# Layer 2 of a four-layer graph kernel: both sums of a pair 64 features wide side by side, the 65th factor in a PSUM bank of its own, and no idle matmuls from layer 1 on

## The chip, the cores and the metric

The kernel runs on one core of a Trainium2 chip. Its engines are TensorE (PE, with its weight loads shown apart as PEld), VectorE (DVE), ScalarE (ACT), GpSimd (POOL) and SyncE (SP, which issues most DMAs). TensorE takes its operands from SBUF and writes to PSUM, which has banks of 512 fp32 columns on 128 partitions. The metric is the device time of one execution in microseconds; the kernel before has a median of 1097.2 us over 3 runs.

## What is computed

`x` is 4096 x 64, `adj` a sparse 4096 x 4096 matrix whose pattern is symmetric and whose values are not. Four layers follow one another, each `x = x + layer(relu(layernorm(x)), adj)`. The change concerns layer 2 alone, aggregation on the Poincare ball:

```python
deg = jnp.maximum(adj.sum(axis=1, keepdims=True), 1e-08)
w = adj / deg
log_ij = _logmap(x[:, None, :], x[None, :, :], c)
agg = jnp.einsum('ij,ijc->ic', w, log_ij)
transformed = agg @ weight + bias
```

`log_ij` is, for every pair (i, j), a vector made of x_i and x_j with factors that depend on the pair. The kernel doesn't form the vectors. It finds one number t_ij for each pair (from the distance of the two points, so that t_ij = t_ji), weighs it by the adjacency, and sums over j the 64 features h_j of the scaled point and one further number z_j. So the sum for a row i has 65 entries: 64 features and a 65th factor. A short chain for each block of 512 rows makes `agg` out of them.

Layer 0 is `relu((adj @ h) @ W0.T + b)`, layer 1 is attention with a sigmoid of products q k, layer 3 counts the non-zeros of each row and weighs by powers of two.

## The kernel before

**Tiles.** 4096 rows are 8 blocks of 512 (W, NB) or 32 chunks of 128 (P, NC). A tile of the adjacency is 2 chunks of j (a group, G = 2) by 512 columns of i, 512 KB. Layers 0, 1 and 3 walk over 8 x 16 such tiles. Layer 2 uses the symmetry of t: its list `work` (line 1058) holds the block pairs (ib, J) with J >= ib, two halves each, 72 entries in all. 16 of them are on the diagonal (ib = J); the 56 others (`two`, listed in `twos`) serve both ways: t itself for the rows of block ib, and t transposed for the rows of block J. In what follows an entry is a *step*, its *own sum* goes to block ib and its *mirrored sum* to block J.

**Engines in a step of layer 2.** In the order of the data:
- `l2_dists` (line 1101): TensorE, products `LT`, `RT` (64 rows) and `LB`, `RB` (32 rows) into one of two PSUM tiles `mm`
- `l2_squares` (1120): ScalarE, `v = mm^2`
- `l2_clamps`, `l2_clamps_v` (1130, 1137): GpSimd clamps `v`; in 30 steps ("shared") it does 768 of the 1024 columns and VectorE does 256
- `l2_signs` (1146): TensorE, a small product on 2 rows
- `l2_first_logs`, `l2_roots`, `l2_inverses` (1157 to 1180): ScalarE, a logarithm and two exponentials
- `l2_coshs` (1182): VectorE, `t = max(mm, ..) + t`, after which the `mm` tile is free; `l2_logs` (1189): ScalarE; `l2_pairs` (1195): VectorE, the finished t
- `l2_weights` (1202): VectorE, `w = t * adj`
- `l2_turns` (1213): TensorE, 8 transposes of t into the two spare banks `tr`; `l2_weights2` (1246): VectorE, `w2 = tr * adj2`
- `l2_sums` (1278): TensorE, own sum, two matmuls of 512 columns
- `l2_sums2` (1299): TensorE, mirrored sum, four matmuls of 256 columns for each half
- `l2_gathers` (1316): after both halves of a block J, the mirrored sum is added to the store `others` (ScalarE for ib = 0, else VectorE).

The stationary operand of both sums is `HA`, 65 columns wide (64 features and the factor), and the sums lie on 65 partitions: the own one in bank `acc0`, the mirrored one in bank `acc1`. All of it is fp32, and every fp32 matmul but a transpose stands as two records in the profile.

After the last step of a block ib, `after2` (line 658) adds the own sum and what was gathered for that block (VectorE), transposes the 65 x 512 result by row (`by_row`, line 384), and goes on with a chain of small operations on all engines; `before3` follows it.

**What sets the order.** The program is written out by a planner (`in_turn`, line 778): every stage is a thread that says on which engine its next piece goes and when its inputs will be there, by a cost model (`Pace`, line 67), and the piece that can start first is issued next. Within layer 2 `in_steps` (line 1329) fixes the order of the stages on each engine. On TensorE, step for step: distances of the next entry, signs, mirrored sum (two entries behind), transposes (one behind), own sum (one behind). Chains such as `after2` are in a queue `tail` and go in between. An engine executes its instructions in the order of issue.

**Idle matmuls.** Where the planner expects TensorE to wait for 0.6 us or longer, `keep_warm` (line 793) issues products of the identity into a spare bank. It does so in layer 0 until the first attention product of layer 1 has been issued, and again from the loading of layer 2's tables until `third_part` (line 1383) opens layer 3. `third_part` also frees layer 2's buffers, `others` among them.

**Side by side.** Layer 0 and the first part of layer 1 use `pair_sum` (line 913): its two matmuls are 64 wide and go to partitions 0 to 63 and 64 to 127 of one bank. The rest of layer 1 uses `quarter_sum` (line 1021) with four products of 64 rows by 64 columns. Layer 3's counts (line 1425) have products `pick` of 128 rows by 32 columns in bf16, four to a bank.

Of the kernel before, what the change touches and what calls it, by code (L numbers as in the profile page):

```python
# [9 lines left out]
F32 = mybir.dt.float32  # L10
# [4 lines left out]
ALU = mybir.AluOpType  # L15
# [131 lines left out]
def kernel(ctx: ExitStack, tc: tile.TileContext, a: dict, out: bass.AP):  # L147
# [79 lines left out]

    HA = keep.tile([P, NC, D + 1], F32, name="HA")  # L230
    RT = keep.tile([P, N], F32, name="RT")
    LT = keep.tile([P, NC // 2, P], F32, name="LT")
    RB = keep.tile([P, N], BF16, name="RB")
# [26 lines left out]
    def later_constants():  # L260


        def patterns():
            yield "POOL", lambda: 60.0
            for t, one in [(t, 1.0) for t in rbs] + [(t, 0.25) for t in lbs]:
                POOL.memset(t, 0.0)
                for k in (1, 3):
                    POOL.memset(t[:, :, k, 1:2], one)

        def weights_of_ranks():  # L270


            yield "DVE", lambda: 150.0
            near_f = st["rows"].tile([P, P], F32, name="near_f", bufs=1)
# [25 lines left out]

        return patterns(), weights_of_ranks()
# [189 lines left out]
    def before2(ib, st):  # L491
# [30 lines left out]
        ACT.copy(HA[:, cs(ib), 0:D], hh[:, :, 0, :])  # L522
# [8 lines left out]
        DVE.tensor_add(HA[:, cs(ib), D : D + 1], v[:, :, 0, :], v[:, :, 1, :])  # L531
        for k in range(3):
            t = rt("r_t", [P, CB, 2, 1], BF16)
            DVE.tensor_copy(t, v)
# [120 lines left out]
        DVE.tensor_add(x[:, cs(ib), :], x[:, cs(ib), :], s)  # L655
        yield ON_V

    def after2(ib, acc, others, st):

        e = rows.tile([P, W], F32, tag="e", name="e")[0 : D + 1, :]  # L660
        if others is None:
            ACT.copy(e, acc[0 : D + 1, :])
        else:
            DVE.tensor_add(e, acc[0 : D + 1, :], others)
        st["acc_free"][0] = pace.latest
        ps = yield from by_row(e, D + 1)

        t = rt("l2", [P, CB, D])  # L670
        z = rt("r_n", [P, CB, 1])
        DVE.tensor_copy(z, ps[:, :, D : D + 1])
        h = HA[:, cs(ib), 0:D]
        hz = rt("r_sq", [P, CB, D])
        DVE.tensor_mul(hz, h, ps[:, :, 0:D])
        DVE.tensor_mul(t, ps[:, :, 0:D], Qc[:, cs(ib), :].to_broadcast([P, CB, D]))
# [8 lines left out]
        DVE.tensor_sub(t, t, hz)  # L685
        vT = columns[slot["now"]]
        yield from transposed(t, D, vT[0:D, :])
# [105 lines left out]
    def keep_warm(wait):  # L793


        if wait < WAIT or not spare or l1[0].get("dist") and "tables" not in opened or "third" in opened:
            return
        t = bank()
        cold = not pace.shape
        for _ in range(min(int((wait - 0.2) / 0.28), 24)):  # L800
            PE.matmul(
                t[:, 0:P], ident, x[:, 0:2, :].rearrange("p c d -> p (c d)") if cold else ident,
                start=True, stop=True,
            )
        emptied(t)


    st = {
        "h0": HA[:, :, 0:D],
        "dg": {}, "dg_done": {}, "acc_free": [0.0, 0.0], "dg_free": [0.0, 0.0],  # L810
    }
    rows_at = {}
    opened = {}
# [269 lines left out]
    def second_part():  # L1083
# [9 lines left out]
        w2["others"] = w2["pool"].tile([D + 1, N], F32, name="others", bufs=1)  # L1093
        opened["second"] = l1[-1]["summed"]

    def second_tables():
# [179 lines left out]
            d["weighed2"] = pace.latest  # L1276

    def l2_sums():
        for d in work:
            yield "PE", lambda: latest(d.get("weighed"), take(0, d))  # L1280
            if d["first"]:
                accs["l2"] = acc_tile(0)
                st["acc_free"][0] = None
            acc = accs["l2"]
            for c in range(G):
                PE.matmul(
                    acc[0 : D + 1, :], HA[:, d["g"] * G + c, :], d["w"][:, c, :],
                    start=(d["first"] and c == 0), stop=(d["last"] and c == G - 1),
                )
            d["summed"] = pace.latest  # L1290
            if d["last"]:
                ib = d["ib"]
                others = w2["others"][:, ws(ib)] if ib else None
                follow(
                    with_mark(3, ib, after2(ib, acc, others, st), before3(ib, None)),
                    ON_V if ib else ON_S, evicts=True,
                )

    def l2_sums2():
        for d in twos:  # L1300
            yield "PE", lambda: latest(
                d.get("weighed2"), 0.0 if d["half"] else st["acc_free"][1]
            )
            if d["half"] == 0:
                accs["turned"] = acc_tile(1)
                st["acc_free"][1] = None
            acc = accs["turned"][0 : D + 1, :]
            part = slice(d["half"] * G * P, (d["half"] + 1) * G * P)
            for k in range(CB):
                PE.matmul(  # L1310
                    acc[:, part], HA[:, d["ib"] * CB + k, :], d["w2"][:, k, :],
                    start=(k == 0), stop=(k == CB - 1),
                )
            d["summed2"] = pace.latest

    def l2_gathers():
        for d in twos:
            if d["half"] == 0:
                continue
            yield "DVE" if d["ib"] else "ACT", lambda: d.get("summed2")  # L1320
            o, acc = w2["others"][:, ws(d["J"])], accs["turned"][0 : D + 1, :]
            if d["ib"] == 0:
                ACT.copy(o, acc)
            else:
                DVE.tensor_add(o, acc, o)
            st["acc_free"][1] = pace.latest
            d["gathered"] = pace.latest

    def in_steps(*stages):
# [197 lines left out]
    def l3_sum():  # L1527
# [15 lines left out]
        if d["last"]:  # L1543
# [67 lines left out]
```

## Time and profile before

| what | value |
|---|---|
| median of 3 runs | 1097.2 us (1095.84 to 1097.63) |
| the profiled execution | 1093.92 us, span 1092.2 us, mean granted TensorE clock 0.988 |
| TensorE busy | 1038.4 us, 95% |
| VectorE busy | 929.7 us, 85% |
| ScalarE busy | 790.0 us, 72% |
| GpSimd busy | 260.2 us, 24% |
| layer 2's stretch, 459 to 905 us | TensorE 428.75, VectorE 410.93, ScalarE 382.56, GpSimd 179.62 of 446 us |
| layer 3's stretch, 905 to 1092 us | TensorE 178.02, VectorE 109.46, ScalarE 138.66, GpSimd 3.38 of 187 us |

How to read the lines below. A line of a timeline has the start in us from the span's start, the length in us, engine, source line, operation, written tile <- read tiles, shape and number of records merged into it; in brackets the idle time of that engine before it and what ended it. All operations go through one helper, so they all show line 139 and are told apart by their tiles. In a shape, `128*65` before a TensorE record is rows by columns of the stationary operand. A line of a stretch has start:end and its length, then busy time and number of instructions of PE, PEld, DVE, ACT and POOL, the granted TensorE clock (1.00 is full), the busy share of the DMA engines and their GB/s. A line of groups ends in busy time (union), mean ns of one, and the idle time ahead of it. TensorE's records overlap, and their ends are modelled, so distances between starts say more than lengths.

### The profile page before, as it was taken

The numbers are of one execution on the slowest core, as the hardware profiler recorded it, in microseconds if no ns is written. First come the engines' busy times: TensorE is split into PE (matmuls) and PEld (weight loads), VectorE is DVE, ScalarE is ACT, GpSimd is POOL, SyncE is SP. The second block draws the span as 40 slices with busy tenths as digits, with TensorE's granted clock in tenths as the row PEclk, the third lists the DMA queues.
The fourth block names the chain that finished last, engine by engine and source line by source line (L and its number), as shares of the span: only waits on it lengthen the run. The fifth ranks groups of instructions, "written<-read, shape, count | busy, mean of one in ns | idle before, by whom it ended". The sixth has DMA issues, their size and how long they took to land.

```text
span 1092.2 us, 16919 instructions
## 1 busy us (share of the span) xinstructions
PE 1038.4 (95%) x6032; PEld 464.3 (43%) x6032; DVE 929.7 (85%) x1522; ACT 790.0 (72%) x1228; POOL 260.2 (24%) x151
## 2 busy tenths in 40 slices
PE   7989999999999999999999999999999988999998
PEld 3334444333233333354454454444444444454444
DVE  7778999988999999888998999989899999665650
ACT  1144545466777777799989879888798777677776
POOL 3021312110110011243344344334343431000000
PEclk9899999999999999999999999999999999999999
DMA  8999999976687778544553553445536549999950
GB/s 288 405 360 408 398 380 379 310 238 218 208 281 265 240 263 274 171 143 173 181 184 118 179 206 116 174 154 174 174 122 209 191 154 380 376 409 409 410 221 10
DMA packets 76202, 271.77 MB, mean 249 GB/s; under 512 B 9046, under 2 KB 10070, under 8 KB 76118
## 3 DMA queue, kind: packets, MB, share of 16 engines
q1 hardware_dynamic: 75456, 270.57, 68.3%
q8 instruction: 47, 0.77, 0.3%
q14 instruction: 37, 0.30, 0.1%
q10 hardware_dynamic: 662, 0.13, 0.1%
HBM read 269.62 MB, written 1.05 MB: 248 GB/s over the span
## 4 chain that ended last, share of the span: by engine, by line
PE 54%; DVE 21%; issue 8%; ACT 6%; POOL 5%; DMA 4%; SPq 1%; ACTq 0%; DVEq 0%; POOLq 0%
PE acc L139 27%; PE mm L139 17%; PE tr L139 10%; DVE dg L139 5%; POOL v L139 4%; DMA adj<-in_adjT_dram 4%; DVE t L139 4%; DVE w L139 3%; DVE sig L139 3%; ACT sig L139 2%; ACT t L139 1%; ACT lo_sq L139 1%; ACT v L139 1%; DVE h L139 1%; DVE ln_v L139 1%
## 5 line engine op out<-in xcount | busy, mean ns | idle before, releaser
L139 PE MATMUL acc<-w,HA 128*65 128x256 f32 (+1 forms) x736 | 246.2, 470 | 8.6 <-DVE w L139 8.4
L139 POOL TENSOR_SCALAR v<-v 128x1024 f32<-128x1024 f32 (+1 forms) x72 | 171.1, 2376 | 253.3 <-ACT v L139 253.3
L139 ACT ACTIVATE sig<-mm,att_b,att_a 128x1024 f32<-128x1024 f32 x128 | 150.7, 1203 | 57.4 <-PE mm L139 53.5
L139 ACT ACTIVATE wt<-mm,down 128x1024 fp32r<-128x1024 f32 x128 | 136.0, 1110 | 40.0 <-PE mm L139 39.2
L139 DVE TENSOR_TENSOR sig<-sig,adj 128x1024 f32<-128x1024 f32 x128 | 152.7, 1220 | 10.6 <-ACT sig L139 10.4
L139 DVE TENSOR_TENSOR dg<-dg,adj 128x1024 f32<-128x1024 f32 x113 | 137.9, 1221 | 1.6
L139 PE MATMUL mm<-qT,kT 64*64 64x512 f32 (+1 forms) x896 | 130.2, 599 | 6.6 <-ACT sig L139 6.1
L139 PEld LDWEIGHTS acc<-w,HA 128*65 128x65 f32 x736 | 94.2, 138 | 92.0 <-issue 50.1
L139 PE MATMUL acc<-sig,HL 64*64 64x512 f32 (+1 forms) x896 | 130.0, 599 | 1.4 <-DVE sig L139 1.4
L139 PE MATMUL acc<-adj,HA 128*64 128x512 f32 x512 | 125.2, 623 | 5.7 <-DMA adj<-in_adjT_dram 5.4
L139 ACT ACTIVATE v<-v,minus 128x1024 f32<-128x1024 f32 x72 | 79.1, 1098 | 27.4 <-POOL v L139 26.3
L139 DVE SCALAR_TENSOR_TENSOR t<-mm,t 128x1024 f32<-128x1024 f32 x72 | 83.6, 1161 | 14.8 <-PE mm L139 11.0
L139 DVE SCALAR_TENSOR_TENSOR t<-t,v 128x1024 f32<-128x1024 f32 x72 | 83.3, 1157 | 3.4 <-ACT t L139 3.4
L139 DVE TENSOR_TENSOR w<-t,adj 128x1024 f32<-128x1024 f32 x72 | 84.4, 1173 | 1.4
L139 DVE TENSOR_TENSOR w<-tr,adj 128x512 f32<-128x512 f32 x120 | 77.5, 683 | 7.5 <-PE tr L139 7.2
L139 ACT ACTIVATE t<-t 128x1024 f32<-128x1024 f32 x72 | 72.2, 1003 | 12.0 <-DVE t L139 11.9
L139 ACT ACTIVATE v<-mm 128x1024 f32<-128x1024 f32 x72 | 69.6, 967 | 14.0 <-PE mm L139 14.0
L139 PE MATMUL mm<-RT,LT 64*128 64x512 f32 (+1 forms) x288 | 77.9, 618 | 0.0
L139 PE MATMUL acc<-wt,S 128*128 128x512 f32 x256 | 77.1, 426 | 0.6 <-ACT wt L139 0.5
L139 ACT ACTIVATE t<-v 128x1024 f32<-128x1024 f32 x72 | 72.7, 1010 | 2.1
L139 ACT ACTIVATE v<-v 128x1024 f32<-128x1024 f32 x72 | 72.1, 1002 | 0.0
L139 PEld LDWEIGHTS mm<-qT,kT 64*64 64x64 f32 (+1 forms) x896 | 37.8, 140 | 77.8 <-ACT sig L139 36.2
(219 smaller groups left out, 1374.7 us busy)
## 6 DMA issues: line engine op xcount, KB each, us to landing
adj<-in_adjT_dram SPq DMA_DIRECT2D x512, 512.0 KB, 5.4
x<-in_x_dram SPq DMA_DIRECT2D x4, 256.0 KB, 4.6
out_dram<-h SPq DMA_DIRECT2D x8, 128.0 KB, 1.9
W<-in_W_dram ACTq DMA_DIRECT2D x3, 16.0 KB, 3.9
line<-in_b_dram ACTq DMA_DIRECT2D x2, 0.2 KB
W0T<-in_W0T_dram ACTq DMA_DIRECT2D x2, 16.0 KB
line<-in_scale_dram ACTq DMA_DIRECT2D x1, 0.0 KB
line<-in_scale_q_dram ACTq DMA_DIRECT2D x1, 0.0 KB
```

Source lines behind the costliest of these rows:

```text
L139: done = self.tc.keep_in_program_order(getattr(self.engine, op)(*args, **kw))
```

## The change

Layer 2's 65 columns are split. `HA` keeps 64 feature columns. The factor goes to a table `ZA` with 15 columns for each chunk, of which only the eighth is not zero; a window of 8 columns of it, shifted by the block's number r, is a stationary operand that puts the factor's sum for block r on the r-th of 8 partitions and adds zeros to the other seven.

The own sum of a step and the mirrored sum of the step before it are issued together by `l2_sums`; `l2_sums2` is gone. The own sum goes to partitions 0 to 63 of bank `acc0`, the mirrored one to partitions 64 to 127 of the same bank, alternating. Then the same weights are multiplied with the window of `ZA`, in four strips (partitions 0, 32, 64 and 96 on) of bank `acc1`. That bank is set to zero once, by four small products of zeros, and never again: it accumulates over all steps.

`others` becomes 128 partitions tall: gathered sums in the upper half, and `after2` copies the own sum into the lower half (ScalarE) instead of adding. It copies the factor bank too (VectorE). In place of the four transposes come four matmuls with `twice` (two identities, one above the other, which add the two halves) and four with a column of `row_of`, which adds up the four strips of a block's factor. `third_part` waits for these products. `keep_warm` stops for good with the first attention product of layer 1. The core of the diff:

```diff
-    HA = keep.tile([P, NC, D + 1], F32, name="HA")
+    HA = keep.tile([P, NC, D], F32, name="HA")
+    ZA = keep.tile([P, NC, 2 * NB - 1], F32, name="ZA")
+    twice = keep.tile([P, D], F32, name="twice")
+    row_of = keep.tile([P, NB], F32, name="row_of")
+    nothing = keep.tile([1, P], F32, name="nothing")
...
-    def after2(ib, acc, others, st):
-
-        e = rows.tile([P, W], F32, tag="e", name="e")[0 : D + 1, :]
-        if others is None:
-            ACT.copy(e, acc[0 : D + 1, :])
-        else:
-            DVE.tensor_add(e, acc[0 : D + 1, :], others)
+    def after2(ib, acc, zacc, st):
+
+        k = P if ib else D
+        e = w2["others"][0:k, ws(ib)]
+        ACT.copy(e[0:D, :], acc[0:D, :])
         st["acc_free"][0] = pace.latest
-        ps = yield from by_row(e, D + 1)
-
-
-
-        t = rt("l2", [P, CB, D])
+        yield ON_V
+        ez = rows.tile([P, W], F32, tag="e", name="e")
+        DVE.tensor_copy(ez, zacc)
+        st["acc_free"][1] = pace.latest
+        yield TURN
+        t = bank()
+        ps, n = t[:, 0 : CB * D].rearrange("p (c k) -> p c k", k=D), CB * D
+        for c in range(CB):
+            b = slice(c * P, (c + 1) * P)
+            PE.matmul(ps[:, c, :], e[:, b], twice[0:k, :], start=True, stop=True)
+            PE.matmul(
+                t[:, n + c : n + c + 1], ez[:, b], row_of[:, ib : ib + 1], start=True, stop=True
+            )
+        opened["rows2", ib] = pace.latest
+        yield ON_V
...
-        if wait < WAIT or not spare or l1[0].get("dist") and "tables" not in opened or "third" in opened:
+        if wait < WAIT or not spare or l1[0].get("dist"):
             return
...
     def l2_sums():
-        for d in work:
-            yield "PE", lambda: latest(d.get("weighed"), take(0, d))
+        for n, d in enumerate(work):
+            turned = work[n - 1] if n and work[n - 1]["two"] else None
+            yield "PE", lambda: latest(
+                d.get("weighed"), take(0, d), st["acc_free"][1],
+                turned.get("weighed2") if turned else 0.0,
+                st["turned_free"] if turned and turned["half"] == 0 else 0.0,
+            )
+            if n == 0:
+                accs["l2"], accs["z"] = acc_tile(0), acc_tile(1)
+                for c in range(CB):
+                    PE.matmul(
+                        accs["z"][:, c * P : (c + 1) * P], nothing, ones_row, start=(c == 0), stop=False,
+                        skip_group_check=True,
+                    )
+            acc, z = accs["l2"], accs["z"]
             if d["first"]:
-                accs["l2"] = acc_tile(0)
                 st["acc_free"][0] = None
-            acc = accs["l2"]
-            for c in range(G):
+            own = [
+                (c, slice(0, W), d["g"] * G + c, d["ib"], d["w"][:, c, :], c == 0 and d["first"],
+                 c == G - 1 and d["last"]) for c in range(G)
+            ]
+            moved = []
+            if turned:
+                if turned["half"] == 0:
+                    st["turned_free"] = None
+                part = slice(turned["half"] * G * P, (turned["half"] + 1) * G * P)
+                moved = [
+                    (G + k // 2, part, turned["ib"] * CB + k, turned["J"], turned["w2"][:, k, :], k == 0,
+                     k == CB - 1) for k in range(CB)
+                ]
+            for c, cols, j, _, w, start, stop in own[0:1] + moved[0:2] + own[1:2] + moved[2:4]:
+                to = slice(D, P) if c >= G else slice(0, D)
+                PE.matmul(acc[to, cols], HA[:, j, :], w, start=start, stop=stop, skip_group_check=True)
+            for c, cols, j, r, w, _, _ in own + moved[0:3:2] + moved[1:4:2]:
                 PE.matmul(
-                    acc[0 : D + 1, :], HA[:, d["g"] * G + c, :], d["w"][:, c, :],
-                    start=(d["first"] and c == 0), stop=(d["last"] and c == G - 1),
+                    z[c * Q : c * Q + NB, cols], ZA[:, j, NB - 1 - r : 2 * NB - 1 - r], w,
+                    start=False, stop=(n == len(work) - 1), skip_group_check=True,
                 )
...
-            o, acc = w2["others"][:, ws(d["J"])], accs["turned"][0 : D + 1, :]
+            o, acc = w2["others"][D:P, ws(d["J"])], accs["l2"][D:P, :]
...
-        yield "ANY", lambda: latest(work[-1].get("summed"), twos[-1].get("gathered"), st["acc_free"][0])
+        yield "ANY", lambda: latest(work[-1].get("summed"), twos[-1].get("gathered"), opened.get(("rows2", NB - 1)))
...
-            (l2_dists(), -1, once), (l2_signs(), 0, once), (l2_sums2(), 2, if_two(1)),
+            (l2_dists(), -1, once), (l2_signs(), 0, once),
             (l2_turns(), 1, lambda d: 2 if d["two"] else 1), (l2_sums(), 1, once),
```

More of the change, by code (lines that the diff above doesn't have):

```diff
@@ L264, in patterns @@
             yield "POOL", lambda: 60.0
+            POOL.memset(ZA, 0.0)
+            POOL.memset(nothing, 0.0)
             for t, one in [(t, 1.0) for t in rbs] + [(t, 0.25) for t in lbs]:
@@ L273, in weights_of_ranks @@
             yield "DVE", lambda: 150.0
+            DVE.tensor_add(twice, ident[:, 0:D], ident[:, D:P])
+            DVE.tensor_reduce(
+                row_of, ident.rearrange("p (q r) -> p r q", q=4)[:, 0:NB, :], AX.X, ALU.add
+            )
             near_f = st["rows"].tile([P, P], F32, name="near_f", bufs=1)
@@ L521, in before2 @@
         ACT.copy(hh[:, :, 1, :], hh[:, :, 0, :])
-        ACT.copy(HA[:, cs(ib), 0:D], hh[:, :, 0, :])
+        ACT.copy(HA[:, cs(ib), :], hh[:, :, 0, :])
         l = rt("l2", [P, CB, D])
@@ L530, in before2 @@
         DVE.tensor_mul(v[:, :, 1, :], n, ic)
-        DVE.tensor_add(HA[:, cs(ib), D : D + 1], v[:, :, 0, :], v[:, :, 1, :])
+        DVE.tensor_add(ZA[:, cs(ib), NB - 1 : NB], v[:, :, 0, :], v[:, :, 1, :])
         for k in range(3):
@@ L656, in after1 @@
         yield ON_V
-    def after2(ib, acc, others, st):
-        e = rows.tile([P, W], F32, tag="e", name="e")[0 : D + 1, :]
-        if others is None:
-            ACT.copy(e, acc[0 : D + 1, :])
-        else:
-            DVE.tensor_add(e, acc[0 : D + 1, :], others)
-        st["acc_free"][0] = pace.latest
-        ps = yield from by_row(e, D + 1)
-        t = rt("l2", [P, CB, D])
+    def after2(ib, acc, zacc, st):
+        k = P if ib else D
+        e = w2["others"][0:k, ws(ib)]
+        ACT.copy(e[0:D, :], acc[0:D, :])
+        st["acc_free"][0] = pace.latest
+        yield ON_V
[13 more added lines that the diff above has]
+        yield ON_V
+        l = rt("l2", [P, CB, D])
         z = rt("r_n", [P, CB, 1])
-        DVE.tensor_copy(z, ps[:, :, D : D + 1])
-        h = HA[:, cs(ib), 0:D]
+        DVE.tensor_copy(z, t[:, n : n + CB].unsqueeze(2))
+        h = HA[:, cs(ib), :]
         hz = rt("r_sq", [P, CB, D])
-        DVE.tensor_mul(hz, h, ps[:, :, 0:D])
-        DVE.tensor_mul(t, ps[:, :, 0:D], Qc[:, cs(ib), :].to_broadcast([P, CB, D]))
+        DVE.tensor_mul(hz, h, ps)
+        DVE.tensor_mul(l, ps, Qc[:, cs(ib), :].to_broadcast([P, CB, D]))
         yield ON_V
@@ L684, in after2 @@
         DVE.tensor_mul(hz, h, z.to_broadcast([P, CB, D]))
-        DVE.tensor_sub(t, t, hz)
+        DVE.tensor_sub(l, l, hz)
         vT = columns[slot["now"]]
-        yield from transposed(t, D, vT[0:D, :])
+        yield from transposed(l, D, vT[0:D, :])
         ps = yield from times(vT, W2, D, ON_S)
@@ L808 @@
     st = {
-        "h0": HA[:, :, 0:D],
-        "dg": {}, "dg_done": {}, "acc_free": [0.0, 0.0], "dg_free": [0.0, 0.0],
+        "h0": HA,
+        "dg": {}, "dg_done": {}, "acc_free": [0.0, 0.0], "turned_free": 0.0, "dg_free": [0.0, 0.0],
     }
@@ L1092, in second_part @@
         w2["pool"] = w2["stack"].enter_context(tc.tile_pool(name="w2", bufs=2))
-        w2["others"] = w2["pool"].tile([D + 1, N], F32, name="others", bufs=1)
+        w2["others"] = w2["pool"].tile([P, N], F32, name="others", bufs=1)
         opened["second"] = l1[-1]["summed"]
@@ L1278, in l2_sums @@
     def l2_sums():
-        for d in work:
-            yield "PE", lambda: latest(d.get("weighed"), take(0, d))
+        for n, d in enumerate(work):
[11 more added lines that the diff above has]
+                        skip_group_check=True,
+                    )
+            acc, z = accs["l2"], accs["z"]
@@ L1289, in l2_sums @@
                 )
             d["summed"] = pace.latest
+            if turned:
+                turned["summed2"] = pace.latest
             if d["last"]:
+                st["acc_free"][1] = None
                 ib = d["ib"]
-                others = w2["others"][:, ws(ib)] if ib else None
                 follow(
-                    with_mark(3, ib, after2(ib, acc, others, st), before3(ib, None)),
-                    ON_V if ib else ON_S, evicts=True,
-                )
[L1299 to L1314, printed above, removed]
+                    with_mark(3, ib, after2(ib, acc, z, st), before3(ib, None)), ON_S, evicts=2,
+                )
@@ L1325, in l2_gathers @@
                 DVE.tensor_add(o, acc, o)
-            st["acc_free"][1] = pace.latest
+            st["turned_free"] = pace.latest
             d["gathered"] = pace.latest
```

## The prediction

> **What bounds it now.** The change touches layer 2 alone (459 to 905 us), so I look for the limit there. The page's first line makes TensorE (PE) the busiest engine over the whole span:
>
> ```profile
> PE 1038.4 (95%) x6032; PEld 464.3 (43%) x6032; DVE 929.7 (85%) x1522; ACT 790.0 (72%) x1228; POOL 260.2 (24%) x151
> ```
>
> A share is no bound, so next I read the busy times of a stretch inside the layer, and then TensorE's timeline over one step (a step is one entry of `work`):
>
> ```profile
> 660.00:720.00 60.00, 58.17 (x287) 28.95 (x286) 57.25 (x72) 53.29 (x61) 24.99 (x12) 1.00 0.45 156
> ```
>
> ```profile
> 690.51 1.88 PE L139 MATMUL acc<-w,HA 128*65 128x512 f32 x4
> 692.32 1.13 PE L139 MATMUL mm<-RT,LT 64*128 64x512 f32 x4
> 693.38 0.39 PE L139 MATMUL mm<-RB,LB 32*128 32x512 bf16 x4
> 693.71 1.94 PE L139 MATMUL acc<-w,HA 128*65 128x256 f32 x8
> 695.49 1.04 PE L139 MATMUL tr<-ident,t 128*128 128x128 f32 x8
> 696.36 1.88 PE L139 MATMUL acc<-w,HA 128*65 128x512 f32 x4
> ```
>
> Each group starts before the modelled end of the one ahead of it; no wait stands between them. A step takes 5.85 us (690.51 to 696.36) and is TensorE's work: own sum 1.81, distances 1.06, small products 0.33, mirrored sum 1.78, transposes 0.87. ScalarE's timeline says the same from the other side:
>
> ```profile
> 693.82 1.02 ACT L139 ACTIVATE v<-mm 128x1024 f32<-128x1024 f32 x1 [0.35 <-PE mm L139]
> ...
> 697.08 1.15 ACT L139 ACTIVATE v<-v,minus 128x1024 f32<-128x1024 f32 x1 [0.35 <-POOL v L139]
> ...
> 699.66 1.02 ACT L139 ACTIVATE v<-mm 128x1024 f32<-128x1024 f32 x1 [0.34 <-PE mm L139]
> ```
>
> The square waits 0.35 us for TensorE's distances in every step. By the starts of the squares, 21 of the 72 steps have this form (5.73 to 5.85 us apart). They are the steps in which GpSimd clamps 768 columns only. The other pair steps clamp 1024 (2.77 us) and are 6.03 us or longer.
>
> **What comes second.** Before TensorE saturates, at 522, one such step runs without its wait:
>
> ```profile
> 522.00 1.01 ACT L139 ACTIVATE v<-mm 128x1024 f32<-128x1024 f32 x1
> 523.09 2.12 POOL L139 TENSOR_SCALAR v<-v 128x768 f32<-128x768 f32 x1 [3.27 <-ACT v L139]
> 525.27 1.14 ACT L139 ACTIVATE v<-v,minus 128x1024 f32<-128x1024 f32 x1
> 526.45 1.06 ACT L139 ACTIVATE t<-v 128x1024 f32<-128x1024 f32 x1
> 527.41 1.00 ACT L139 ACTIVATE v<-mm 128x1024 f32<-128x1024 f32 x1
> ```
>
> This is a ring: square, clamp, logarithm, root, next square, each behind the other: 1.09 + 2.18 + 1.18 + 0.96 = 5.41 us. With the clamp of 1024 columns it is 0.64 longer, 6.05, which is what those steps take now: a faster TensorE gives them nothing. VectorE is next: its rows in two steps from 690.28 are busy 5.61 us (with a gather) and 5.58 (without one, but with 0.82 instead of 0.41 in the small clamp, which starts right behind GpSimd's). The extra 0.41 looks like waiting inside the instruction; without it the mean is (5.61 + 5.17) / 2 = 5.39. So both floors lie at 5.4, and 0.45 us of a step is the most that TensorE can give.
>
> **Part 1, the sums.** Now both sums have 65 output columns and run one matmul at a time: each 512-column record starts 0.43 us after the one before (690.51, 690.94, 691.37). The change makes them 64 wide, puts the mirrored sum into the upper half of the bank, and repeats both with 8 columns for the 65th factor. The trace has the two shapes' neighbours:
>
> ```profile
> L139 PE MATMUL acc<-w,HA 128*65 128x512 f32 x288 | 137.9, 602 | 7.3 <-DVE w L139 7.2
> L139 PE MATMUL acc<-w,HA 128*65 128x256 f32 x448 | 108.3, 385 | 1.3 <-DVE w L139 1.2
> L139 PE MATMUL acc<-adj,HA 128*64 128x512 f32 x512 | 125.2, 623 | 5.7 <-DMA adj<-in_adjT_dram 5.4
> L139 PE MATMUL acc<-sig,HL 64*64 64x512 f32 x768 | 99.4, 599 | 1.4 <-DVE sig L139 1.4
> ```
>
> Layer 0 puts two 64-wide products side by side: 125.2 / 512 = 0.245 us a record. Layer 1 runs four tiles: 99.4 / 768 = 0.129. Both means include the gaps at a change of shape. Counted in 512-column records, a pair step has 4 for its own sum, 4 for the mirrored one (8 of 256 columns), and 8 for the factor. After: 8 x 0.245 + 8 x 0.129 = 1.96 + 1.03 = 2.99 us against 1.81 + 1.78 = 3.59: **0.60 less**, so TensorE needs 5.25 a step and stops being the bound.
>
> Two things in this are not in the trace. A 512-column product beside two of 256 columns: bounds 4 turns of 0.43 (full overlap) and 6 (each pair waits for its longer member). And 8 columns wide, 128 rows, fp32, four abreast: bounds 0.129 (layer 1, four tiles of 64 rows) and 0.43 a record (one at a time); layer 3's `pick` products have the very tile, 128*32, in bf16, and 16 of them take 1005.42 to 1006.40, 0.061 each against 0.43 / 2 alone, so four abreast works there. I take 0.129, the nearest in width and type.
>
> The Trainium skill, "TensorEngine Tiling (Array Packing)", Key Properties, speaks against this: changing the tiling mode drains the engine, and the change adds two modes to a step. The trace shows the drain: own sum's last record to distances is 692.32 - 691.80 = 0.52 instead of 0.43. At about 0.14 for entry and first record, two more changes are 0.28; on bare rates (8 x 0.215 + 8 x 0.107 = 2.58) that gives 2.86 instead of 2.99. The same skill, "TensorE: Matmul & The Clock Gate", Measured speedup vs the span model, has three column tiles gain 2.38 times, not 3: by that estimate the factor's part is 0.86 / 0.79 = 1.09.
>
> What it is worth: a step goes from 5.85 to about 5.45 (floors 5.39 and 5.41, not perfectly meshed; ends 5.41 and 5.80). 21 x 0.40 = **-8.4**. At the turn of a row block the square waits 1.48 us for TensorE (at 722.63); five such turns get 0.60 each: **-3.0**.
>
> **Part 2, what is added beside it.** A sum without a mirrored partner (16 of 72) pays 4 factor records with only two abreast, 4 x 0.245 = 1.0 us. These stand at the turns, where TensorE is busy 4.3 to 5.6 us of 6.5 to 7.1; zero on the path, 16 at worst. after2 changes 4 transposes (0.46) for 16 matmul records, 0.9 us: 8 x 0.45, covered likewise. It moves one 512-column copy to ScalarE (0.57 x 7), in the wait of 1.48 just named; 4.0 if that cover is gone. VectorE copies the factor bank (0.69) where it added the gather (0.68). One sum now waits for its own weights, the former step's mirrored weights and, at a new column block, the gather; the distances are queued behind it and the square behind those. Mirrored weights end at 691.57, own at 694.43; the merged sum would start after the transposes, about 694.7. The gather is due a step earlier: no new stall, 0.3 us of room. Memsets and the two small tables stand at 60 and 150 us, outside every wait: nothing.
>
> **Part 3, no idle matmuls.** They are 138 records (19.6 us busy), put by the planner into TensorE's waits. Four bursts of 14 (1.5 us each at 597, 680, 752, 812) stand on the chain, right ahead of saturated steps; their worth is already in part 1. What they buy is the clock:
>
> ```profile
> 465.90:469.30 3.40, 2.54 (x21) 2.34 (x22) 2.18 (x7) 3.40 (x5) 1.49 (x1) 1.00 1.01 381
> ...
> 841.70:845.10 3.40, 2.01 (x15) 1.36 (x16) 3.33 (x6) 3.31 (x6) 0.00 (x0) 1.00 0.55 176
> 845.10:848.50 3.40, 3.40 (x6) 0.60 (x5) 3.33 (x8) 2.71 (x5) 3.00 (x2) 0.50 0.49 154
> ```
>
> After a stretch with TensorE busy 2.01 of 3.40 the clock (seventh figure behind the stretch's length: 0.50) is halved for 3.4 us, and four sum records at 844.91 take 3.53 instead of 1.94: 1.6 lost. At 465.90 idle matmuls held it. I expect two or three more such stretches (layer 2's first 15 us, some turns), half of the loss hidden: **+1.6** (bounds -2, since bursts vanish, and +8 for five in full).
>
> **Sum.** -8.4 - 3.0 + 1.6 = -9.8. The profiled run took 1093.92 us (span 1092.2 and 1.7 around it), so 1084.1; the median of the runs shown, 1097.2, lies 3.3 above it, and I carry that: **1087.4**.
>
> **Rivals.**
> A: VectorE or the ring holds the step near 5.80. For it: VectorE is busy 57.25 of 60 us. Against: its 5.39 without the inflated clamp. Gain 21 x 0.05 + 3.0 - 1.6 = 2.5: 1094.7, and 1093 to 1100 with the covers gone.
> B, slower: the narrow factor products don't run four abreast. The price is theirs alone; it decides once they take over 3.59 - 1.96 = 1.63 us a pair step. Two abreast (8 x 0.245 = 1.96): TensorE needs 6.18, +0.33 on 21 steps, +0.13 to 0.15 on some 30 others, +1.0 at some ten sums without a partner, +1.6 clock: about +23, 1120. One at a time (8 x 0.43): 7.66, +1.8 on 21 and +1.6 on 30: some +90, 1187. For it: no fp32 row with 128 rows four abreast. Against: `pick`.
> C: the side by side halves overlap better than layer 0's mean and the head of the layer meshes: 1077 to 1081.
>
> **Chances.** Forecast (1081 to 1093) 0.58, A 0.13, B two abreast or uneven (1100 to 1125) 0.18, B serial 0.05, C 0.06. Low end 1080; the high end 1109 leaves out about half of B. Faster by over 0.2% (2.2 us, about what a measurement of this kernel can tell) means under 1095: the forecast, C and a third of A, 0.67. Within: 0.08. Slower: 0.25.
>
> **What would show it.** In the profile after: 128*64 and 128*32 records (8 columns wide) in layer 2, the first starting in pairs, the second in fours; squares 5.4 to 5.5 us apart, their wait for TensorE gone and one for the clamp in its place; TensorE's share below 95%; a few more halves in its clock. Wrong: squares further apart than 5.85 with TensorE still gapless (B), or 5.8 with VectorE gapless (A).

## The result, and the profile after

| | before | after |
|---|---|---|
| median, four runs each | 1096.5 us (1093.16 to 1097.63) | 1129.8 us (1127.31 to 1133.79) |
| profiled execution | 1093.92 us, span 1092.2 | 1133.79 us, span 1132.1 |
| mean granted TensorE clock | 0.988 | 0.967 |

The ratio is 1.0321 (95% interval 1.0290 to 1.0351): **slower by 33 us**, where 9.8 us faster was forecast. The page of the kernel after, its engines and the row of TensorE's granted clock over 40 slices:

```profile
PE 1041.8 (92%) x6734; PEld 459.4 (41%) x6734; DVE 929.3 (82%) x1525; ACT 793.7 (70%) x1235; POOL 260.6 (23%) x153
...
PEclk9799999999999999889989999999999888999999
```

TensorE's share fell from 95 to 92% in a longer span, and its clock dips in layer 2 (slices 17 to 34). To see where the time went I took the starts of ScalarE's squares, one per step, in both traces:

| stretch of layer 2 | before | after | difference |
|---|---|---|---|
| head: steps (0,0,0) to (0,4,1) | 62.6 | 75.9 | +13.3 |
| the other 6 steps of block 0 | 34.5 | 34.6 | +0.1 |
| turns: the first 6 steps of each of blocks 1 to 4 | 147.9 | 161.8 | +13.9 |
| the other 16 steps of these blocks | 115.0 | 107.9 | -7.1 |
| blocks 5 to 7, to layer 3's first `wt` | 79.6 | 93.1 | +13.5 |
| sum | 439.6 | 473.3 | +33.7 |

The sum agrees with the medians. Layer 3 takes 193.2 and 193.4 us. The profiled execution after came to layer 2 6.0 us later as well; in the kernels below this start varies from 457.8 to 466.8 us, so I compare from the first square on.

**What went as forecast** is the fourth row. TensorE and ScalarE in a shared step of the kernel after:

```profile
728.38 1.95 PE L139 MATMUL acc<-w,HA 128*64 128x512 f32 x12 [0.19 <-DVE w L139]
730.26 1.05 PE L139 MATMUL acc<-w,ZA 128*8 128x512 f32 x12
731.24 1.13 PE L139 MATMUL mm<-RT,LT 64*128 64x512 f32 x4
732.30 0.39 PE L139 MATMUL mm<-RB,LB 32*128 32x512 bf16 x4
732.62 1.09 PE L139 MATMUL tr<-ident,t 128*128 128x128 f32 x8
733.65 1.95 PE L139 MATMUL acc<-w,HA 128*64 128x512 f32 x12
```

```profile
727.35 1.00 ACT L139 ACTIVATE v<-mm 128x1024 f32<-128x1024 f32 x1
...
730.59 1.15 ACT L139 ACTIVATE v<-v,minus 128x1024 f32<-128x1024 f32 x1
731.77 1.06 ACT L139 ACTIVATE t<-v 128x1024 f32<-128x1024 f32 x1
732.74 1.02 ACT L139 ACTIVATE v<-mm 128x1024 f32<-128x1024 f32 x1
```

The squares stand 5.39 us apart (5.85 before) and wait for nothing; both sums and the factor take 728.38 to 731.24, 2.86 us instead of 3.59.

**What did not** has three places. *Head.* TensorE, then ScalarE, from step (0,1,0) on:

```profile
473.14 2.08 PE L139 MATMUL mm<-RT,LT 64*128 64x512 f32 x4 [3.13 <-DVE t L139]
...
479.48 0.69 PE L139 MATMUL tr<-ident,lb 128*128 128x128 f32 x2 [1.82 <-ACT lb L139]
483.59 2.07 PE L139 MATMUL acc<-ones_row,nothing 1*128 1x128 f32 x8 [3.43 <-DVE e L139]
485.59 3.67 PE L139 MATMUL acc<-w,HA 128*64 128x512 f32 x4
```

```profile
476.10 1.00 ACT L139 ACTIVATE v<-mm 128x1024 f32<-128x1024 f32 x1
...
482.24 0.57 ACT L139 COPY e<-acc 128x512 f32<-128x512 f32 x1
491.84 1.02 ACT L139 ACTIVATE v<-mm 128x1024 f32<-128x1024 f32 x1 [9.02 <-PE mm L139]
```

The first sum needs the factor's bank, `acc1`, set to zero. Layer 1's last block still lies in it; the copies that take it out (ScalarE `e<-acc`, then VectorE) come at 482.24. Before, the same copy stood at 463.25, and `acc1` was not wanted until the first mirrored sum. The distances of the next step are queued behind the sum: 15.74 us between two squares, 6.05 before. Meanwhile the clock is at half from 472.5 to 489.6, and four sum records take 3.67 us.

*Turns.* The products at a block's end:

```profile
743.74 0.33 PE L139 MATMUL tr<-twice,others 128*128 128x64 f32 x2
744.48 0.38 PE L139 MATMUL tr<-row_of,e 128*128 128x1 f32 x2 [0.40 <-DVE e L139]
744.72 0.41 PE L139 MATMUL tr<-twice,others 128*128 128x64 f32 x2
...
746.13 1.95 PE L139 MATMUL acc<-w,HA 128*64 128x512 f32 x12
```

They take 743.74 to 746.13, 2.4 us, with a wait for VectorE's copy of the factor's bank in it; the four transposes before took 0.4 (722.52 to the next product). Of the six steps of this turn the square-to-square times were 6.05, 5.22, 6.51, 7.11, 6.03, 6.05 and are 6.04, 4.58, 7.12, 8.49, 7.14, 6.05.

*Last blocks.* The step (7,7,0) takes 11.58 us instead of 6.81. TensorE, then ScalarE:

```profile
911.49 0.66 PE L139 MATMUL tr<-ident,t 128*128 128x128 f32 x4
916.51 1.11 PE L139 MATMUL tr<-ident,t 128*128 128x128 f32 x4 [4.37 <-DVE w L139]
917.56 2.98 PE L139 MATMUL acc<-w,HA 128*64 128x512 f32 x4
```

```profile
912.99 1.00 ACT L139 ACTIVATE v<-mm 128x1024 f32<-128x1024 f32 x1
...
916.41 0.56 ACT L139 CAST total<-tr 128x512 bf16<-128x512 f32 x1
916.88 1.15 ACT L139 ACTIVATE v<-v,minus 128x1024 f32<-128x1024 f32 x1
922.82 0.58 ACT L139 CAST chunks<-tr 128x512 bf16<-128x512 f32 x1 [4.79 <-PE tr L139]
```

One spare bank holds the counts of `total` (layer 3's work, done in advance). The copy that frees it stands behind a square and two exponentials, so the transposes of t get one bank instead of two, and TensorE stands still for 4.37 us, until VectorE has read the first half of them out of that bank.

### The profile page after: what moved, and what is told of

Same layout as the page of the kernel before. It is cut to its first block, busy times and chain, and to the rows that moved or that the text cites. A ratio compares the mean times of both kernels' runs of the same rounds, so it can differ in the third digit from the quotient of the medians.

```text
span 1132.1 us, 18331 instructions
## 1 busy us (share of the span) xinstructions
PE 1041.8 (92%) x6734; PEld 459.4 (41%) x6734; DVE 929.3 (82%) x1525; ACT 793.7 (70%) x1235; POOL 260.6 (23%) x153
## 4 chain that ended last, share of the span: by engine, by line
PE 46%; DVE 25%; issue 11%; ACT 9%; POOL 7%; DMA 2%; ACTq 0%; POOLq 0%; DVEq 0%; SPq 0%
PE acc L139 23%; PE mm L139 14%; PE tr L139 9%; POOL v L139 6%; DVE sig L139 5%; DVE dg L139 4%; DVE t L139 4%; DVE w L139 4%; ACT v L139 2%; DMA adj<-in_adjT_dram 2%; ACT t L139 2%; ACT sig L139 1%; DVE r_n L139 1%; DVE others L139 1%; DVE h L139 1%
## 5 line engine op out<-in xcount | busy, mean ns | idle before, releaser
L139 PE MATMUL acc<-w,HA 128*64 128x256 f32 (+1 forms) x736 | 152.3, 505 | 16.7 <-DVE w L139 12.1
L139 PEld LDWEIGHTS acc<-w,HA 128*64 128x64 f32 x736 | 70.2, 145 | 71.0 <-issue 23.0
L139 PE MATMUL tr<-ident,t 128*128 128x128 f32 x480 | 67.3, 281 | 23.2 <-DVE t L139 17.5
L139 PE MATMUL acc<-w,ZA 128*8 128x256 f32 (+1 forms) x736 | 76.1, 468 | 0.0
```

What stands on the lines that cost most here:

```text
L139: done = self.tc.keep_in_program_order(getattr(self.engine, op)(*args, **kw))
```

## The experiments

Theories: **C**, the clock: the loss comes from the idle matmuls that are gone. **W**, the wait for `acc1` at the head. **F**, the factor's own bank: its products, copies and longer chain at the turns. **O**, the order that the planner finds, above all at layer 2's end. Ratios are to the kernel before, from runs on the same chip.

| run | kernel | median us | ratio (95%) |
|---|---|---|---|
| e1 | after, idle matmuls back | 1123.8 | 1.0268 (1.0233 to 1.0302) |
| e2 | before, idle matmuls gone | 1098.0 | 1.0030 (1.0007 to 1.0053) |
| e3 | after, layer 1's copies not held back | 1128.9 | 1.0313 (1.0285 to 1.0342) |
| e4 | e1 + e3 | 1117.5 | 1.0211 (1.0178 to 1.0243) |
| e13 | after, block-end products grouped | 1122.5 | 1.0235 (1.0187 to 1.0284) |
| e6 | e4 + grouped | 1107.5 | 1.0112 (1.0074 to 1.0150) |
| e5 | e4 + block 0's gathers on VectorE | 1114.5 | 1.0163 (1.0115 to 1.0212) |
| e12 | e4 + both | 1105.0 | 1.0091 (1.0062 to 1.0119) |
| e18 | e12, idle matmuls gone again | 1117.1 | 1.0199 (1.0160 to 1.0238) |
| e14 | e12 + W x columns first | 1103.4 | 1.0084 (1.0052 to 1.0117) |
| e8 | e4 without the factor | 1101.3 | 1.0062 (1.0037 to 1.0086) |
| e19 | e8 + gathers, W x columns first | 1090.3 | 0.9960 (0.9935 to 0.9986) |
| e7 | e4 + factor's products split off | 1111.5 | 1.0152 (1.0113 to 1.0190) |
| e9 | e4, nothing of layer 1 held back | 1117.8 | 1.0218 (1.0170 to 1.0266) |
| e11 | e12 + split | 1107.5 | 1.0104 (1.0054 to 1.0154) |
| e15 | e14 + split | 1109.2 | 1.0138 (1.0095 to 1.0181) |
| e16 | e15 + short trains of idle matmuls | 1110.8 | 1.0132 (1.0080 to 1.0184) |

**e1 to e4: clock and held copies.** Edits: the old condition of `keep_warm` into after (e1), the new one into before (e2); and in the planner (e3):

```diff
-                    if "tables" in opened and "weighed" not in work[FIRST]:
+                    if "tables" in opened and "weighed" not in work[FIRST] and not entry["evicts"]:
                         start += 2 * EPS
```

> The changed kernel with the idle matmuls put back into TensorE's waits of layers 1 and 2 as before; everything else of the change stays. Theory C (clock: the loss comes from the idle matmuls that are gone): the 54.6 us of half clock that layer 2 shows after the change go; at half clock TensorE's work takes about twice as long, so at most 27 us come back, about 20 of them on the path: 1107 to 1112 us. Theory W (waits: the first sum needs the bank acc1 that layer 1's last block has not handed on, and the turns of row blocks have a longer chain): the wait of 12 us at the head stays, with the clock full only its 3 to 5 us of slow records come back there, and some 5 elsewhere: 1120 to 1125. Theory F (the factor's own bank costs more work than it saves): 1130, no change.

> The kernel before with the idle matmuls of TensorE's waits taken out from layer 1 on as the change does, and nothing else. Theory C: the loss comes with them, 15 to 25 us, 1112 to 1121. Theory W: without the new waits there are few windows for the clock to drop in: 1097 to 1102. Theory F: 1097, or some us less since each idle matmul stood ahead of a real one.

> The changed kernel; the copies that take layer 1's last block out of its bank are no longer held back behind the first square's chain on ScalarE, and nothing else. Theory W: the first steps of layer 2 lose their wait of 12 us for acc1 (step (0,1,0) 15.7 us, again near 6 to 8) and with it the half clock of that place: 8 to 13 us less, 1117 to 1122. Theory C: the wait goes but the clock falls in other windows all the same: 1122 to 1130. Theory F: 1130 less at most 3.

> The changed kernel with both edits: idle matmuls back, and the copies of layer 1's last block not held back. If theories C and W each have a part of the loss of 33 us, their sum: 1098 to 1108. If C alone holds it is as with the idle matmuls alone, if W alone as with the copies alone. If theory F has most of it, above 1118.

The idle matmuls give 6.0 us back in the changed kernel, no more, and cost the kernel before 2.7 when taken away: C alone falls. The freed copies alone give nothing that can be told (0.8 us); with the idle matmuls they give 6.3. Step (0,1,0) is 15.74, 13.71 (e1), 13.27 (e3), 10.85 us (e4), so wait and clock each have a part of it. In e3 the head is 5.4 us shorter, but turns and quick steps lose 5.0: the clock is now at half in two stretches each of blocks 2 and 3, where the kernel after had full clock:

```profile
664.10:667.50 3.40, 3.40 (x16) 1.49 (x16) 3.17 (x12) 2.21 (x2) 0.85 (x1) 0.50 0.36 128
698.30:701.70 3.40, 3.40 (x18) 1.43 (x18) 3.37 (x6) 3.05 (x4) 1.81 (x1) 0.51 0.63 161
```

From e3 to e4 TensorE's other products keep their order, and the idle matmuls give 11.4 us: that much is the clock. Together the two edits give 12.3 us of 33, where 22 to 32 were expected if clock and wait had the loss between them.

**e8: the factor left out.** The loop over `ZA`, the zeros, the copy `ez` and the `row_of` products are deleted from e4, and a column of the sums is read in place of the factor, so the output differs.

> The changed kernel with idle matmuls back and layer 1's copies not held back (1117.5 us), and the 65th factor left out altogether: no products into its bank, no copy of that bank, no row_of products at the end of a block; the factor read there is a column of the sums instead, so the output differs. Own and mirrored sums side by side stay. Theory F (the factor's own bank is what costs): its 12 records of 1.05 us per pair step, 1.0 in sums without a partner and some 1.5 us of the block's end go; the steps with shared clamp are held by the ring at 5.4 us and gain nothing, so the gain is at the turns and the head: 8 blocks by 2.5 to 4 us, 1085 to 1097. Theory O (the order that the planner finds, at the head and at layer 2's end, is what costs, whatever the factor does): 1106 to 1115.

16 us less, between what F and O forecast. The turns of blocks 1 to 4 fall from 159.5 to 146.5 us (147.9 before), blocks 5 to 7 from 90.9 to 79.2 (79.6 before), the 16 quick steps stay at 107.9. So where the factor is absent there is no loss at the turns, and where TensorE has room (the quick steps) the factor costs nothing: F, with its places. The copy that `after2` moves to ScalarE is still there, so its cover at the turns holds. The planner's order changes with the edit, so the 16 us are the factor and what its absence does to the order. But two steps of block 0 now take 10.55 and 13.39 us, and the kernel is still not faster than before.

**e6, e13: the order of eight products.**

```diff
             PE.matmul(ps[:, c, :], e[:, b], twice[0:k, :], start=True, stop=True)
+        for c in range(CB):
+            b = slice(c * P, (c + 1) * P)
             PE.matmul(
                 t[:, n + c : n + c + 1], ez[:, b], row_of[:, ib : ib + 1], start=True, stop=True
```

> The same kernel of 1117.5 us with the eight products at a block's end in another order: first the four of 64 columns, then the four that pick the factor, so that the first four do not stand behind the copy of the factor's bank. Theory F: the eight records pairs alternate at 0.225 us each and wait 0.40 us once; grouped they take 0.12 each and the wait is covered, 1 to 1.5 us at each of 8 turns, most of it on the path: 1108 to 1113. Theory O: under 2 us from the products themselves, 1115 to 1118, unless the planner's order changes at the end.

> The changed kernel (1129.8 us) with the products at a block's end grouped, four of 64 columns and then four that pick the factor, and nothing else. Theory O (much of the loss is one bad order at layer 2's end: the copy of total stands behind a square on ScalarE while a bank hangs on it, so TensorE stands still for 4.4 us and then works at half clock): the step (7,7,0) falls from 11.6 us to 6 to 7 and the steps after it get faster too, 8 to 12 us less: 1118 to 1122. Theory F (the products themselves): 8 turns by 0.6 us, 1125. Theory C (clock): the half-clock windows of the head stay, 1120 at best.

Without any other edit this gives 7.2 us (e13), on e4 it gives 10.0. The turn of block 3 in e12, which has the edit too:

```profile
721.64 1.00 PE L139 MATMUL tr<-twice,others 128*128 128x64 f32 x8
722.48 1.00 PE L139 MATMUL tr<-row_of,e 128*128 128x1 f32 x8
723.42 1.95 PE L139 MATMUL acc<-w,HA 128*64 128x512 f32 x12
```

1.8 us for what took 2.4, and no wait for the factor's copy. That wait is the whole difference; the alternation costs nothing, as block 5 of the kernel after shows, where the copy is there in time and the alternating products take 1.77 us too:

```profile
857.03 0.33 PE L139 MATMUL tr<-twice,others 128*128 128x64 f32 x2
857.20 0.33 PE L139 MATMUL tr<-row_of,e 128*128 128x1 f32 x2
...
858.80 1.95 PE L139 MATMUL acc<-w,HA 128*64 128x512 f32 x12
```

The step (i,i+1,0) is 6.51 again instead of 7.12 (8.75 at half clock in block 3 of e4) in blocks 2 to 4. That is some 3.8 us at the turns (159.5 to 155.8). Another 5.7 us come from blocks 5 to 7: the planner now finds another order there, with the copy of `total` at 892.25, right after its counts. ScalarE in e6:

```profile
892.25 0.59 ACT L139 CAST total<-tr 128x512 bf16<-128x512 f32 x1 [0.75 <-PE tr L139]
...
894.41 1.01 ACT L139 ACTIVATE v<-mm 128x1024 f32<-128x1024 f32 x1
```

The step (7,7,0) is 6.48 us (14.46 in e4), the one behind it 12.95 (10.99 in e4). So O is real too: an edit of two lines elsewhere moves 8 us in one step and 5.7 in all at the end of the layer. In e13 the step falls only to 9.72, and blocks 5 to 7 gain 4.6. Of the 2.9 us by which e4's step was longer than after's (11.58), the idle matmuls have 1.4: 12 records of them stand ahead of the product that ScalarE waits for. The rest is a half clock that lasts 6.8 us there instead of 3.4.

**e5, e12: block 0's gathers** copied by VectorE instead of ScalarE (`yield "DVE"`, `DVE.tensor_copy(o, acc)`).

> The kernel with idle matmuls back and layer 1's copies not held back (1117.5 us), with the mirrored sums of block 0 copied out by VectorE as in the other blocks, not by ScalarE. The ring of block 0 takes 6.11 us in every step that has this copy, 0.70 above the 5.41 of the others. Theory R (ScalarE's copy stands in the ring between the squares): 6 steps by 0.7, 1113 to 1114. Theory V (VectorE, busy 5.4 of 5.4 us in these steps, takes its place): no change, 1117.

> The same kernel with both: block 0's mirrored sums copied by VectorE and the products at a block's end grouped (alone: 1107.5). The sum of both if theory R holds: 1103 to 1105. If VectorE takes the place of ScalarE in block 0: 1107.

Block 0's last six steps, 34.6 us in e4 with every second step at 6.11, are 32.4 in both, all at 5.39 to 5.44: theory R, the copy in the ring. Once the ring is the bound, a copy of 0.57 us on ScalarE lies in the ring.

**e18: idle matmuls out of e12.**

> The kernel of 1105.0 us with the idle matmuls taken out again from layer 1 on. Theory C (the clock is a cause of its own): 6 us or more come back, 1111 to 1115. Theory W (the clock fell where the new waits were, and these are gone): 1105 to 1108, as for the kernel before, which loses 2.7 us by it.

12 us are lost again, and its page shows the clock falling again. Up to block 5 the order of the program is that of e12, and 8.4 us of the loss lie there; in blocks 5 to 7 the order differs, and their 2.9 us can't be assigned. So the clock is a cause of its own in the changed kernel, 6 to 11 us of it depending on the rest, and 2.7 in the kernel before. The head of e18:

```profile
473.42 2.07 PE L139 MATMUL acc<-ones_row,nothing 1*128 1x128 f32 x8
475.42 3.68 PE L139 MATMUL acc<-w,HA 128*64 128x512 f32 x4
479.02 1.09 PE L139 MATMUL acc<-w,ZA 128*8 128x512 f32 x4
```

The wait for `acc1` is gone, but four records still take 3.68 us.

**e14: the product of W and columns.** A diagonal block's second sum, which has no partner, is held until that product is issued:

```diff
+                opened.get(("times2", d["ib"] - 1)) if d["ib"] and d["cut"] else 0.0,
```

> The kernel with idle matmuls back, layer 1's copies not held back, block 0's mirrored sums copied by VectorE and the end-of-block products grouped (1105.0 us), and now the sum without partner of a block's second step put behind the product of W and columns of the block's end. Theory T (the turn's chain: ScalarE waits 1.34 us for that product at 732.50, and the step is 8.49 us against 7.11 before): the step falls to 7.1 to 7.5 in six blocks: 1097 to 1101. Theory D (the step is then held by the distances that come later for it): 8.2 to 8.5, 1103 to 1105.

ScalarE in e12, then in e14, at the copy of that product:

```profile
730.11 1.05 ACT L139 ACTIVATE t<-t 128x1024 f32<-128x1024 f32 x1
732.50 0.37 ACT L139 COPY hb<-tr 128x256 f32<-128x256 f32 x1 [1.34 <-PE tr L139]
```

```profile
735.25 1.05 ACT L139 ACTIVATE t<-t 128x1024 f32<-128x1024 f32 x1
736.19 0.36 ACT L139 COPY hb<-tr 128x256 f32<-128x256 f32 x1
```

The wait is gone and the step is 7.22 us in place of 8.49, as theory T has it. But a later step of each turn's block goes from 5.39 to 5.82, (1,2,0) took 8.53 us at half clock in this execution, and layer 3 came out 3.8 us longer, about what layer 2 gained (448.7 to 444.6). The median moves by 1.7 us, which the intervals do not tell from nothing.

**e7, e9, e11, e15, e16: misses.** The factor's products as a step of their own (e7, e11, e15), trains of at most 8 idle matmuls (e16), nothing of layer 1 held back (e9).

> The same kernel of 1117.5 us with the factor's products as a step of their own behind the sums, so that the first sum does not wait for acc1 and the planner may set the block end's products between the two. Theory F: the products that stood behind sums without partner come 1.0 us earlier at each turn: 1107 to 1113. Theory W (what is left at the head is still the wait for acc1): the step (0,1,0) loses 2 to 4 us, 1112 to 1116. Theory O: no change beyond 2 us except by a new order at layer 2's end.

> The same kernel of 1117.5 us with none of layer 1's last chains held back behind layer 2's first steps. Theory O: the step (0,1,0), still 10.9 us, waits on TensorE and ScalarE work that came 10 us later than before (the copy of h at 475.99 against 465.29); without the hold it comes early again and the step falls to 6 to 8 us: 1112 to 1115. Theory F: 1117, no change.

> The same as the one before with trains of at most 8 idle matmuls in place of 24. If a train that the planner sized by a wait that did not come was what made one step of block 0 take 13 to 16 us, that step is 6 to 9 us: 1090 to 1097, at or below the kernel before. If the wait is real (a load that lands late), no change.

e7's gain of 6 us comes from the turns (5.5 us) and from the order at the end ((7,7,0) 6.10 us; 5.3 in blocks 5 to 7), less what the head loses: (0,1,0) falls to 8.90 us, but the whole head is 5.9 longer. With the end already mended the split gives nothing: e11 is 2.4 us above e12, e15 5.9 above e14, with overlapping intervals. e15 had been expected at 1093 to 1098, or 1100 to 1106 with a train in the way; e11 at 1098 to 1108. In e7, e11, e15 and e16 one step of block 0 takes 13 to 16 us, as in e8. Shorter trains take it from 15.69 to 13.15 (e15, e16): the train has 2.5 us of it at most. In e16 the next distances stand there behind the transposes for the tables `RB` and `LB` of a later row block, which layer 1's last chain makes. e9 shifts that chain ahead and (0,1,0) falls to 6.33 as expected, but the wait moves to the steps before ((0,0,0) 11.61 us). How the head could be ordered better was not found.

**e19: the mended kernel without the factor.**

> The mended kernel (idle matmuls back, layer 1's copies not held back, block 0's mirrored sums copied by VectorE, the product of W and columns ahead of the sum without partner; 1103.4 us) with the factor left out: no products into its bank, no copy of it and no row_of products, and the factor's value read from a column of the sums, so the output differs. Theory F (the factor's bank eats the gain of the side-by-side sums): 1085 to 1093, below the kernel before by 0.3 to 1%. Theory H (head and end of layer 2 eat it, whatever the factor costs): 1096 to 1103.

1090.3 us, ratio 0.9960, below the kernel before as F has it; with the factor (e14) it is 1.0084. The factor, with the order that goes with it, costs 13 us, in the turns (152.2 against 143.7), the quick steps (109.7 and 107.9), blocks 5 to 7 (83.4 and 79.2) and, less surely, layer 3. The head goes the other way (67.0 and 69.6). No run with the factor beat the kernel before.

## Why the prediction was wrong

The gain that was forecast for the quick steps came; what failed are terms that were put at nothing or too small, at the head, at the turns and at the layer's end.

- **The bound and the floors**: right. TensorE was the limit of the shared steps, and they fell to 5.39 to 5.41, the floor of the ring.
- **Part 1's sizes**: right. 2.99 us were forecast and 2.86 measured: 1.88 for the sums (12 records), so a 512-column product beside two of 256 overlaps fully, and 0.98 for the factor, four abreast.
- The Trainium skill's rules that spoke against the change, weighed in part 1: "TensorEngine Tiling (Array Packing)", Key Properties, says that a change of mode drains the engine; with 0.14 us for each change the estimate was 2.86, which is what this trace has. "TensorE: Matmul & The Clock Gate", Measured speedup vs the span model, gives a gain of 2.38 for three column tiles; the estimate from it, 1.09 for the factor, lies above the measured 0.98.
- **"21 x 0.40 = -8.4"**: 16 of these steps gave 7.1. The rest, in block 0, gave nothing: there ScalarE also copies the gathers (0.57 us), which the ring of 5.41 us leaves out. That copy had been covered by the wait for TensorE that the change removes (e5: 2.1 us).
- **"five such turns get 0.60 each"**: the wait at (i,i+1,0) did shrink (5.22 to 4.58), and the next three steps lost 0.61, 1.38 and 1.11. The failing words are *covered likewise*. The 16 records of after2 were sized at 0.9 us. They start 0.11 us apart, grouped or not, and take 1.77, and with the copy of the factor's bank not there in time 2.39; the four transposes took 0.4, not 0.46. And the sum without a partner was judged by TensorE's free time at the turn, not by what is queued behind it: W x columns, and ScalarE behind that (e14). The turns cost 13.9 us more, not 3.0 less.
- **"The gather is due a step earlier: no new stall"**: I checked the merged sum's wait in a steady step and not in the first one, where the second bank has another owner. Head +13.3; the held copies and the clock have 9.5 of it (e4: 66.4 against 75.9).
- **"+1.6 (bounds -2 and +8)"** for the clock: mis-sized. Layer 2, up to layer 3's first `wt`, has 47.8 us at half clock after and 3.4 before (the 54.6 of e1's expectation takes in one stretch behind it). The idle matmuls are worth 6.0 us alone (e1), 11.4 with the copies freed (e3 to e4). I counted windows in the old trace, but the change itself leaves TensorE less busy and so makes new ones.
- **Not in the forecast at all**: the end of layer 2, 13.5 us longer, of which one step has 4.8. Another order there gave 5.7 us of it back (e6); without the factor there was no loss (e8: 79.2 us against 79.6 before).
- **Rivals**: A, B and C did not happen. I looked for the slower side in the new products' rate; it came from the terms that were put at zero.

Open: how the loss at the turns divides among the factor's products, the copy and the sum without partner, beyond the 0.6 us a turn of e6 and the 1.3 of e14; why the planner places `total` and layer 1's last chains as it does, and what is left at the head (4.4 us in e12).

## What to carry to other kernels

A cost that looks covered is covered by a certain wait: if the same change removes that wait, the cost is back, so price it against the new bound. When a change lets a second bank be needed earlier, look at who owns it at the first use, not in a steady step. Where a planner writes the order, a small edit moves microseconds at far places: read the steps one by one, and do not judge a mechanism by the total.

## What the runs showed of the hardware

The clock fell without a long idle time. TensorE in two pairs of stretches of the kernel after (the clock is the third figure from the end):

```profile
585.20:588.60 3.40, 1.98 (x14) 1.10 (x12) 3.37 (x4) 3.09 (x5) 0.72 (x1) 1.00 0.70 272
588.60:595.40 6.80, 6.80 (x25) 4.68 (x25) 4.72 (x13) 2.83 (x3) 2.04 (x1) 0.50 0.53 175
803.70:807.10 3.40, 3.00 (x26) 2.40 (x24) 3.30 (x5) 2.53 (x4) 1.62 (x1) 0.99 0.91 359
807.10:810.50 3.40, 3.40 (x13) 1.73 (x13) 3.23 (x11) 2.19 (x2) 1.14 (x1) 0.50 0.49 149
```

In the first the longest gap is 0.78 us; in the third the records cover 3.00 of 3.40 us and the clock is halved all the same. Most of that stretch is the block-end products of 64 columns and of one column, a record every 0.11 us. In e12, where they are grouped and the idle matmuls are back, the clock is 1.00 all through layer 2. With one of the two edits it still fell: in e4 (not grouped) in the turn of block 3, from 732.9 to 736.3, and in e13 (no idle matmuls) in that of block 4, from 821.8 to 825.2. What sets the clock is not shown by these runs. The Trainium skill, "TensorE: Matmul & The Clock Gate", Why this matters for your kernels, asks for no gap over some 3 us between bursts; here that was not enough.
